# A fused pre-norm transformer block: the first norm moved behind the projections of queries, keys and values

## Chip, cores, metric

The kernel runs on one core of one Trainium2 chip. The metric is the device time of one execution in microseconds (us). All data is float32.

## What is computed

A block of attention and feed-forward over 16 sequences of 256 tokens with 256 features and 16 heads of 16.

```python
def _layernorm(x, axis=-1, eps=1e-05):
    m = jnp.mean(x, axis=axis, keepdims=True)
    v = jnp.var(x, axis=axis, keepdims=True)
    return (x - m) / jnp.sqrt(v + eps)

# attention, on xn = _layernorm(x); heads of 16
q, k, v = (xn @ wq.T), (xn @ wk.T), (xn @ wv.T)            # split into 16 heads
scores = einsum('bihd,bjhd->bhij', q, k) * 16 ** -0.5
scores = where(j - i > 16, -inf, scores)
x = x + einsum('bhij,bjhd->bihd', softmax(scores), v) @ wo.T

# feed-forward, on xn = _layernorm(x); gate_w, up_w (1024 x 256) and down_w (256 x 1024)
# are cubic splines through 2033 control points each
x = x + (silu(xn @ gate_w.T) * (xn @ up_w.T)) @ down_w.T
```

## The kernel before

One sequence is one block of work ("block b": 256 tokens as two chunks of 128 partitions). The main loop (L647) runs over 20 stages `s`. Stage `s` overlaps five blocks: in it the maxima of the scores are searched for block `nb = s - 1`, the exponentials are made for `tb = s - 2`, attention is finished and projected for `ob = s - 3`, the feed-forward part is done for `s - 3` and `s - 4`, and the projections of queries, keys and values are made ahead of need: in stages from 4 on for block `s + 2`, and in stages 0 to 3, where the pipeline fills, by a table (`projections`, L599) that names stage and gap.

A stage has four `inner` and two `outer` steps that multiply queries and keys into two PSUM tiles (`scores`), which DVE (`find_max`, tiles `z` and `mx`) and ACT (`e`, exponentials) read. Between them are gaps numbered 1 to 7, and other work is put into the gaps: `project(s, gap)` for the norm and the projections, `fill(s, gap)` for the feed-forward products (`pg`, `pu`, `pd`) and, in stages 0 to 3, for making the dense weights from the splines (`pw`) and for idle products (`run`, `keep_running`) that only keep TensorE running.

Every engine executes in the order in which the program is written: `InOrder` (L78) records each instruction with that demand, so all of them carry L88 in the profile, and the reader goes by tile names. SP's queue of DMAs is held to the same order: a DMA that waits holds those behind it.

The first norm of block b goes through these steps:

- `load_x` (L126) brings the block in, tile `x`, ten buffers.
- `stats_a` (`norm_stats`, L191): mean and variance on DVE (`statsa`, `mva`), the power -1/2 on GpSimd (`rstda`).
- `norm_a` (L228): two DVE instructions subtract the mean and multiply (`xna`).
- `turn_a` (L231, `transposed`, L212): four TensorE transposes into a PSUM tile (`pta`), and one ACT copy to SBUF (`xnT`).
- `project_qk` (L235): eight matmuls (16 records in the profile) into `pq` and `pk`; ACT copies them to `qkc`, the queries scaled by 16 ** -0.5.
- `spread` (L252): eight DMAs move `qkc` to the layout `qk` that the score products read, four heads at 32-row offsets. Block 0's go half by SP and half by ACT, all others by SP.
- `project_v` (L262): four matmuls into `pv`, two ACT copies into `v`.

When all maxima of a block are found, `turn_max` (L387) transposes them (`pm`, `mxT`), and four DMAs write them as an extra row into `qk`; the products for the exponentials of the next stage subtract the maxima through that row. Every stage of the attention's end has DMAs on SP as well: sums (`den`), heads (`ac`), reciprocals out and back in 16 copies (`rd`, `rb`).

The PSUM tiles tagged `m` have two buffers; `pta`, `pq`, `pk`, `pv`, `po`, `py`, `ptf` (the second norm's transposes) and `pm` take turns in them.

Of the kernel before, what the change touches and what calls it, by code (L numbers as in the profile page):

```python
# [18 lines left out]
P = 128  # L19
# [74 lines left out]
def block_kernel(  # L94
    ctx: ExitStack,
    tc: tile.TileContext,
    x: bass.AP,
    wqT: bass.AP,
    wkT: bass.AP,
    wvT: bass.AP,  # L100
# [11 lines left out]
    const = ctx.enter_context(tc.tile_pool(name="const", bufs=1))  # L112
    sb = ctx.enter_context(tc.tile_pool(name="sb", bufs=2))
    sb1 = ctx.enter_context(tc.tile_pool(name="sb1", bufs=1))
    sb4 = ctx.enter_context(tc.tile_pool(name="sb4", bufs=4))
    sb6 = ctx.enter_context(tc.tile_pool(name="sb6", bufs=6))
    sbx = ctx.enter_context(tc.tile_pool(name="sbx", bufs=10))
# [5 lines left out]

    xs = {}

    def load_x(b, engine):  # L126
        xs[b] = sbx.tile([P, 2, DIM], F32, tag="x", name=f"x{b}")
        engine.dma_start(xs[b], x[b].rearrange("(c p) d -> p c d", p=P))

    AHEAD = 2  # L130
    load_x(0, sp)
    w_in = {}
    for nm, src in (("q", wqT), ("k", wkT), ("v", wvT), ("o", woT)):
        t = const.tile([P, 2, DIM], F32, tag=f"w{nm}", name=f"w{nm}")
        act.dma_start(t, src.rearrange("(kc p) o -> p kc o", p=P))
        w_in[nm] = t
    load_x(1, sp)
    tab_in = const.tile([P, NPART + 2 * P], F32, tag="tab", name="tab_in")
    sp.dma_start(tab_in, tab)
    cp_in = const.tile([P, 3, NPART], F32, tag="cp", name="cp_in")  # L140
    second_in = const.tile([P, 2, NROW], mybir.dt.uint8, tag="second", name="second_in")
    for w in range(3):
        sp.dma_start(cp_in[:, w, :], cps[w])
        if w == 0:
            load_x(2, sp)
            sp.dma_start(second_in, second)
    load_x(3, sp)


    ident = const.tile([P, P], F32, tag="ident", name="ident")  # L150
    make_identity(nc, ident)
    neghalf = const.tile([P, 2], F32, tag="neghalf", name="neghalf")
    pool.memset(neghalf, -0.5)
    mask0 = const.tile([P, JB], F32, tag="mask0", name="mask0")
    mask1 = const.tile([P, S], F32, tag="mask1", name="mask1")
    masks = (mask0, mask1)
# [26 lines left out]
    downT = const.tile([P, 8, DIM], F32, tag="downT", name="downT")  # L183


    xns, xnTs, mxs, aus, aos, recs, x2s, x2Ts = ({} for _ in range(8))
    es, inters, qkcs = {}, {}, {}

    moments = {}
# [1 line left out]
    def norm_stats(b, nm):  # L191
        stats = sb.tile([P, 2, 6], F32, tag=f"stats{nm}", name=f"stats{nm}{b}")
        mv = sb.tile([P, 2, 2], F32, tag=f"mv{nm}", name=f"mv{nm}{b}")
        for c in range(2):
            dve.bn_stats(stats[:, c, :], xs[b][:, c, :])
            dve.bn_aggr(mv[:, c, :], stats[:, c, :])
        rstd = sb.tile([P, 2], F32, tag=f"rstd{nm}", name=f"rstd{nm}{b}")
        dve.tensor_scalar_add(rstd, mv[:, :, 1], EPS)
        pool.tensor_tensor(rstd, rstd, neghalf, ALU.pow)
        moments[b, nm] = mv, rstd  # L200

    def normed(b, nm):
        mv, rstd = moments.pop((b, nm))
        xn = sb.tile([P, 2, DIM], F32, tag=f"xn{nm}", name=f"xn{nm}{b}")
        for c in range(2):
            dve.tensor_scalar(
                xn[:, c, :], xs[b][:, c, :], mv[:, c, 0:1], rstd[:, c : c + 1],
                ALU.subtract, ALU.mult,
            )
        return xn  # L210
# [14 lines left out]
    def stats_a(b):  # L225
        norm_stats(b, "a")

    def norm_a(b):  # L228
        xns[b] = normed(b, "a")

    def turn_a(b):  # L231
        xnTs[b] = sb.tile([P, 2, S], F32, tag="xnT", name=f"xnT{b}")
        transposed(xns.pop(b), xnTs[b], f"ta{b}")

    def project_qk(b):  # L235
        qkcs[b] = qkc = sb.tile([P, 2, 2, S], F32, tag="qkc", name=f"qkc{b}")
        for i, nm in enumerate("qk"):
            pq = ps_m.tile([P, 2, S], F32, tag="m", name=f"p{nm}{b}")
            for oc in range(2):
                for kc in range(2):  # L240
                    pe.matmul(
                        pq[:, oc, :],
                        lhsT=w_in[nm][:, kc, oc * P : (oc + 1) * P],
                        rhs=xnTs[b][:, kc, :],
                        start=(kc == 0),
                        stop=(kc == 1),
                    )
            act.activation(
                qkc[:, i], pq, AF.Copy, scale=HD**-0.5 if nm == "q" else 1.0
            )  # L250

    def spread(b):  # L252
        qkc = qkcs.pop(b)
# [8 lines left out]
    def project_v(b):  # L262
        pv = ps_m.tile([P, 2, DIM], F32, tag="m", name=f"pv{b}")
        for c in range(2):
            for kc in range(2):
                pe.matmul(
                    pv[:, c, :],
                    lhsT=xnTs[b][:, kc, c * P : (c + 1) * P],
                    rhs=w_in["v"][:, kc, :],
                    start=(kc == 0),  # L270
                    stop=(kc == 1),
                )
        for c in range(2):
            act.copy(
                vs[b % NQK][:, c, :, 0:HD],
                pv[:, c, :].rearrange("p (h d) -> p h d", d=HD),
            )
        del xnTs[b]

# [41 lines left out]
    def inner(nb, tb, g):  # L323
# [11 lines left out]
            scores(qt, False, g, 0, 0, S)  # L335
        def exponentials(pr):
            e = sb6.tile([P, 2, S], F32, tag="e0", name=f"e0{tb}_{g}_{pr}")
            act.activation(e, tiles[pr][:, :, 0:S], AF.Exp)

            pool.affine_select(  # L340
                out=e[:, :, 0:M0], in_=e[:, :, 0:M0],
                compare_op=ALU.is_ge, fill=0.0, base=LOOK,
                pattern=[[0, 2], [1, M0]], channel_multiplier=-1,
            )
            es[tb, 0, g, pr] = e
# [7 lines left out]
    def outer(nb, tb, g2):  # L353
# [10 lines left out]
        def exponentials(pr):  # L364
# [4 lines left out]
                    :, :, :, W0 - W1 : W0  # L369
                ],  # L370
                AF.Exp,
            )
            pool.affine_select(
                out=e[:, :, :, 0:P], in_=e[:, :, :, 0:P],
# [95 lines left out]
        norm_stats(b, "f")  # L470

    def norm_f(b):
        x2s[b] = normed(b, "f")

    def turn_f(b):
        x2Ts[b] = sb.tile([P, 2, S], F32, tag="x2T", name=f"x2T{b}")
# [79 lines left out]
    def do(stage, b, *args):  # L556
        if 0 <= b < B:
            stage(b, *args)

    heads = {
        (0, 7): (0, 6),
        (1, 1): (1, 0), (1, 4): (1, 2), (1, 5): (1, 2), (1, 6): (0, 5), (1, 7): (0, 5),
        (2, 1): (1, 0), (2, 3): (1, 6), (2, 5): (1, 1), (2, 6): (0, 4),
        (3, 3): (0, 5), (3, 6): (0, 6),
    }
    parts = iter([(w, part) for part in range(2) for w in range(2)] + [(2, 0), (2, 1)])

    def keep_running(n):
        run = ps_f.tile([P, 2 * S], F32, tag="f", name="run")
# [2 lines left out]

    def fill(s, gap):

        n, idle = heads.get((s, gap), (0, 0))
        if idle:
            keep_running(idle)  # L580
        for _ in range(n):
            spline(*next(parts))

        alone = s > B
        late = s >= B - AHEAD
        for what, at in (
            ((gate_up, s - 4, 1), 1),
            ((gate_up, s - 4, 2), 2 if late else 3),
            ((gate_up, s - 4, 3), 3 if late else 4),
            ((down, s - 4, 0), 4 if alone else 5),  # L590
            ((down, s - 4, 1), 5 if alone else 6),
            ((gate_up, s - 3, 0), 7),
        ):
            if at == gap:
                do(*what)

    projections = {  # L599
        (0, 1): ((stats_a, 1),),  # L600
        (0, 2): (
            (norm_a, 1), (coefficients, 0), (coefficients, 1), (stats_a, 2),
            (scores_and_values, 1), (scores_and_values, 2), (project_qk, 0), (spread, 0),
        ),
        (0, 4): ((turn_a, 1), (norm_a, 2)),
        (0, 6): ((project_v, 0),),
        (1, 1): ((turn_a, 2), (coefficients, 2)),
        (1, 2): ((project_qk, 1), (spread, 1)),
        (1, 3): ((project_qk, 2), (spread, 2), (scores_and_values, 3)),
        (1, 6): ((project_v, 1),),  # L610
        (1, 7): ((stats_a, 3), (norm_a, 3), (project_v, 2)),
        (2, 1): ((turn_a, 3), (stats_a, 4), (scores_and_values, 4)),
        (2, 2): ((norm_a, 4), (project_qk, 3), (spread, 3)),
        (2, 4): ((turn_a, 4),),
        (2, 6): ((project_v, 3),),
        (2, 7): ((stats_a, 5), (norm_a, 5), (project_qk, 4)),
        (3, 1): ((turn_a, 5), (stats_a, 6)),
        (3, 2): ((norm_a, 6), (spread, 4), (project_qk, 5), (spread, 5)),
        (3, 3): ((project_v, 4),),
        (3, 4): ((turn_a, 6),),  # L620
        (3, 6): ((project_v, 5),),
    }

    def project(s, gap):
        if s < 4:
            todo = projections.get((s, gap), ())
        else:
            pb = s + AHEAD
            todo = {
                1: ((stats_a, pb + 1),),  # L630
                2: ((norm_a, pb + 1), (project_qk, pb), (spread, pb)),
                4: ((turn_a, pb + 1),),
                6: ((project_v, pb),),
            }.get(gap, ())
        for stage, b in todo:
            do(stage, b)


    for t in tiles:
# [2 lines left out]
    scores_and_values(0)  # L642
    constants()
    stats_a(0)
    norm_a(0)
    turn_a(0)
    for s in range(B + 4):  # L647
        nb, tb, ob = s - 1, s - 2, s - 3
        inner(nb, tb, 0)
# [4 lines left out]
        inner(nb, tb, 1)  # L654
        do(invert, ob)
        if s + 2 + AHEAD < B:
            load_x(s + 2 + AHEAD, sp)
        project(s, 2)
        fill(s, 2)
        outer(nb, tb, 0)  # L660
# [7 lines left out]
        inner(nb, tb, 3)  # L668
        do(project_o, ob)
        do(stats_f, ob)  # L670
        fill(s, 5)
        do(norm_f, ob)
        outer(nb, tb, 1)
        fill(s, 6)
        do(turn_f, ob)
        project(s, 6)
        do(turn_max, nb)
        project(s, 7)
        fill(s, 7)
# [29 lines left out]
```

## Time and profile before

| | us |
|---|---|
| median of 3 runs | 671.82 (671.68 to 675.86) |
| profiled execution | 670.9 |
| its span, first to last instruction | 669.2 |
| busy: TensorE / weight loads / VectorE / ScalarE / GpSimd | 652.2 / 511.6 / 358.5 / 230.3 / 128.1 |

The span begins with the first instruction and ends with the last, so the execution's time is a little longer. PE is TensorE's matmuls, PEld its weight loads, DVE VectorE, ACT ScalarE, POOL GpSimd, SP the engine that issues most DMAs (SPq is its queue). A row `349.93 0.59 PE pta L88 x4` of the chain of waits is start, duration, engine, tile, line, number of records; in the timeline the operation and its tiles follow. In the table by stretches of time the columns are stretch, length, and for PE, PEld, DVE, ACT and POOL busy time and instructions, then TensorE's granted clock, the share of the DMA engines, and GB/s.

### The profile page before, as it was taken

What the parts mean: (1) busy time and instruction counts of PE and PEld (TensorE: products, weight loads), DVE (VectorE), ACT (ScalarE), POOL (GpSimd) and SP (SyncE); (2) the same over time, 40 slices, a digit from 0 to 9 for tenths busy, and PEclk for the clock granted to TensorE, in tenths of its full rate; (3) what the DMA queues carried; (4) which work ended last, traced back from release to release, by engine and by line L of the source; (5) the groups of instructions that cost most, each with busy time, mean ns of one, the idle gap of its engine ahead of it and who ended that gap; (6) DMA issues with size and microseconds to landing.
All of it is one profiled execution on the core that took longest, in us unless ns stands there. A gap on an engine that the chain in (4) does not pass through costs nothing.

```text
span 669.2 us, 18583 instructions
## 1 busy us (share of the span) xinstructions
PE 652.2 (97%) x7484; PEld 511.6 (76%) x7484; DVE 358.5 (54%) x1473; ACT 230.3 (34%) x413; POOL 128.1 (19%) x250
## 2 busy tenths in 40 slices
PE   7999989999999999999999999999999999999998
PEld 6666767877778787777878777787877777776876
DVE  6576556556464645645464564545455565623332
ACT  2345434243342424334242433423233333333110
POOL 5222212111121211112121121211112121212000
PEclk9999999999999999999999999999999999999999
DMA  8422142113030210313031121303010101010100
GB/s 253 64 40 35 37 82 61 35 23 66 24 77 19 66 33 20 65 27 73 20 72 27 22 63 27 59 19 62 22 30 24 25 14 36 18 45 24 34 17 16
DMA packets 34422, 29.65 MB, mean 44 GB/s; under 512 B 7840, under 2 KB 33696, under 8 KB 34336
## 3 DMA queue, kind: packets, MB, share of 16 engines
q1 hardware_dynamic: 32928, 27.15, 18.1%
q10 hardware_dynamic: 1408, 1.31, 0.7%
q8 instruction: 59, 0.97, 0.6%
q14 instruction: 27, 0.22, 0.1%
HBM read 10.88 MB, written 4.46 MB: 23 GB/s over the span
## 4 chain that ended last, share of the span: by engine, by line
PE 94%; ACT 2%; DVE 2%; DMA 1%; issue 1%; POOL 0%; SPq 0%; ACTq 0%; DVEq 0%
PE pg L88 18%; PE pd L88 17%; PE pu L88 17%; PE scores L88 14%; PE po L88 6%; PE pq L88 5%; PE py L88 5%; PE pk L88 4%; PE pv L88 4%; PE pta L88 1%; PE ptf L88 1%; PE run L88 1%; PE pw L88 1%; ACT e L88 1%; DMA qk<-qkc 1%
## 5 line engine op out<-in xcount | busy, mean ns | idle before, releaser
L88 ACT ACTIVATE e<-scores 128x512 f32<-128x512 f32 (+1 forms) x192 | 117.4, 615 | 252.2 <-PE scores L88 188.5
L88 DVE CUSTOM_DVE_ANT_0 z<-scores,mask 128x144 bf16<-128x144 f32 (+1 forms) x512 | 154.4, 362 | 71.4 <-PE scores L88 36.7
L88 POOL TENSOR_SCALAR_AFFINE_SELECT e<-e 128x224 f32<-128x224 f32 (+1 forms) x192 | 94.6, 493 | 421.4 <-ACT e L88 420.9
L88 PE MATMUL pg<-x2T,gateT 128*128 128x256 f32 x512 | 125.1, 387 | 2.8 <-ACT x2T L88 2.8
L88 PE MATMUL pu<-x2T,upT 128*128 128x256 f32 x512 | 121.0, 379 | 0.0
L88 PE MATMUL pd<-downT,inter 128*128 128x256 f32 x512 | 117.0, 382 | 0.0
L88 DVE SCALAR_TENSOR_TENSOR th<-th,pg 128x512 f32<-128x512 f32 x64 | 44.0, 687 | 132.7 <-ACT th L88 132.7
L88 PEld LDWEIGHTS pg<-x2T,gateT 128*128 128x128 f32 x512 | 92.3, 190 | 21.2 <-ACT x2T L88 4.2
L88 PE MATMUL scores<-qk 17*64 17x144 f32 (+7 forms) x4096 | 105.7, 317 | 2.2 <-ACT e L88 1.1
L88 PEld LDWEIGHTS pu<-x2T,upT 128*128 128x128 f32 x512 | 97.3, 190 | 13.2
L88 PEld LDWEIGHTS pd<-downT,inter 128*128 128x128 f32 x512 | 96.1, 190 | 14.0 <-issue 0.2
L88 PEld LDWEIGHTS scores<-qk 17*64 17x64 f32 (+1 forms) x4096 | 68.6, 131 | 37.8 <-issue 29.2
L88 ACT ACTIVATE th<-pg 128x512 f32<-128x512 f32 x64 | 38.2, 597 | 69.7 <-PE pg L88 69.2
L88 DVE TENSOR_TENSOR inter<-th,pu 128x512 f32<-128x512 f32 x64 | 44.0, 688 | 26.1 <-PE pu L88 26.1
L88 PE MATMUL po<-e,v 128*32 128x256 f32 (+1 forms) x1024 | 50.0, 335 | 0.1
L88 PEld LDWEIGHTS po<-e,v 128*32 128x32 f32 x1024 | 29.6, 109 | 23.3 <-issue 12.5
L88 DVE DVE_READ_ACCUMULATOR2_ANT mx<- 128x1 f32 x512 | 42.2, 82 | 0.0
L88 DVE TENSOR_TENSOR x<-x,pd 128x256 f32<-128x256 f32 x32 | 13.5, 421 | 51.9 <-PE pd L88 51.9
L88 PE MATMUL pq<-xnT,wq 128*128 128x256 f32 x128 | 31.9, 392 | 1.2 <-ACT xnT L88 0.7
L88 PE MATMUL py<-wo,ac 128*128 128x256 f32 x128 | 31.8, 391 | 1.1 <-ACT e L88 1.1
L88 PE MATMUL pv<-wv,xnT 128*128 128x256 f32 x128 | 30.6, 382 | 0.8 <-ACT v L88 0.6
L88 PEld LDWEIGHTS py<-wo,ac 128*128 128x128 f32 x128 | 23.1, 189 | 9.5 <-issue 4.6
(54 smaller groups left out, 414.7 us busy)
## 6 DMA issues: line engine op xcount, KB each, us to landing
qk<-qkc SPq DMA_DIRECT2D x124, 64.0 KB
x<-x SPq DMA_DIRECT2D x16, 256.0 KB
ac<-au SPq DMA_DIRECT2D x128, 32.0 KB
rb<-rd SPq DMA_DIRECT2D x32, 128.0 KB
out<-x SPq DMA_DIRECT2D x15, 256.0 KB
qk<-mxT SPq DMA_DIRECT2D x64, 4.0 KB
den<-au SPq DMA_DIRECT2D x64, 4.0 KB
cp_in<-cps SPq DMA_DIRECT2D x3, 256.0 KB
```

Of the source, the lines that this page charges most:

```text
L88: return self.tc.keep_in_program_order(fn(*args, **kwargs))
```

## The change

With `xn = (x - m) * r`, a projection `xn @ w.T` equals `r * (x @ wc.T)`, where `wc` is `w` with the mean over its input features taken off. So the changed kernel multiplies the raw input with centred weights, and brings in `r` later:

- The host also gives `xT`, each block transposed. `load_xT` fetches it, three buffers, and `norm_a` and `turn_a` are gone for blocks 1 to 15. Block 0 alone keeps norm and transposes (`norm_first`) and uses the weights as they are.
- `sum_weights` multiplies each of the three weights with a matrix of 1/256 (the column means, spread over all partitions), `center` takes them off in place on DVE.
- Values: the ACT copy takes the token's factor as its scale. Queries and keys: tokens lie along the free axis, so `r` is needed in all partitions. `send_factors` writes it to DRAM (`ra`, 128 x 2 single numbers), `spread_factors` reads it back into all partitions (`fa`, 128 x 256), and DVE multiplies `pq` and `pk` by it, in place of ACT's copies.
- The scale 16 ** -0.5 moves into the exponentials.
- The table of stages 0 to 3 is written anew, with idle products and spline parts in it; in stage 3 `project_v` comes ahead of `turn_f`.

```diff
+    sb3 = ctx.enter_context(tc.tile_pool(name="sb3", bufs=3))
...
+    def load_xT(b):
+        xTs[b] = sb3.tile([P, 2, S], F32, tag="xT", name=f"xT{b}")
+        sp.dma_start(xTs[b], xT[b].rearrange("(kc p) t -> p kc t", p=P))
...
+    sp.dma_start(cp_in[:, 0, :], cps[0])
+    load_x(2)
+    load_xT(1)
+    sp.dma_start(second_in, second)
+    sp.dma_start(cp_in[:, 1, :], cps[1])
+    load_xT(2)
+    load_x(3)
+    sp.dma_start(cp_in[:, 2, :], cps[2])
...
+    def norm_first():
+        xTs[0] = sb3.tile([P, 2, S], F32, tag="xT", name="xT0")
+        transposed(normed(0, "a", "f"), xTs[0], "ta0")
...
+    def sum_weights(nm):
+        sums[nm] = ps_f.tile([P, DIM], F32, tag="f", name=f"sum{nm}")
+        for kc in range(2):
+            pe.matmul(
+                sums[nm], lhsT=means, rhs=w_in[nm][:, kc, :], start=(kc == 0), stop=(kc == 1)
+            )
+    def center(nm):
+        for kc in range(2):
+            dve.tensor_tensor(
+                w_in[nm][:, kc, :], w_in[nm][:, kc, :], sums[nm], ALU.subtract
+            )
+    def send_factors(b):
+        _, factors[b] = moments.pop((b, "a"))
+        across[b] = dr.tile([S], F32, tag="ra", name=f"ra{b}")
+        sp.dma_start(across[b].rearrange("(c p) -> p c", p=P), factors[b])
+    def spread_factors(b):
+        to = sb3.tile([P, S], F32, tag="fa", name=f"fa{b}")
+        sp.dma_start(to, across[b].unsqueeze(0).to_broadcast([P, S]))
+        across[b] = to
     def project_qk(b):
...
-                        rhs=xnTs[b][:, kc, :],
+                        rhs=xTs[b][:, kc, :],
...
-            act.activation(
-                qkc[:, i], pq, AF.Copy, scale=HD**-0.5 if nm == "q" else 1.0
-            )
+            if b == 0:
+                act.copy(qkc[:, i], pq)
+            else:
+                dve.tensor_tensor(
+                    qkc[:, i], pq, across[b].unsqueeze(1).to_broadcast([P, 2, S]), ALU.mult
+                )
     def project_v(b):
...
-            act.copy(
+            act.activation(
                 vs[b % NQK][:, c, :, 0:HD],
                 pv[:, c, :].rearrange("p (h d) -> p h d", d=HD),
-            )
+                AF.Copy,
+                scale=1.0 if b == 0 else factors[b][:, c : c + 1],
+            )
...
-            act.activation(e, tiles[pr][:, :, 0:S], AF.Exp)
+            act.activation(e, tiles[pr][:, :, 0:S], AF.Exp, scale=HD**-0.5)
...
+    early = {
+        (0, 1): ((stats_a, 1), (send_factors, 1)),
+        (0, 2): (
+            (project_qk, 0), (spread, 0), (center, "q"), (sum_weights, "k"), (coefficients, 0),
+            (stats_a, 2), (scores_and_values, 1), (scores_and_values, 2),
+        ),
+        (0, 6): (
+            (project_v, 0), (sum_weights, "v"), (center, "k"), (center, "v"), (keep_running, 1),
+            (spread_factors, 1), (send_factors, 2), (spread_factors, 2),
+        ),
+        (1, 1): ((part, 0), (coefficients, 1)),
+        (1, 2): ((project_qk, 1), (spread, 1)),
+        (1, 3): ((project_qk, 2), (spread, 2), (coefficients, 2), (scores_and_values, 3)),
+        (1, 4): ((keep_running, 2), (part, 1)),
+        (1, 5): ((keep_running, 2), (part, 2)),
+        (1, 6): ((keep_running, 5), (project_v, 1)),
+        (1, 7): (
+            (stats_a, 3), (send_factors, 3), (spread_factors, 3), (keep_running, 4),
+            (project_v, 2), (keep_running, 1),
+        ),
+        (2, 1): ((part, 3), (stats_a, 4), (send_factors, 4), (scores_and_values, 4)),
+        (2, 2): ((project_qk, 3), (spread, 3), (spread_factors, 4)),
+        (2, 3): ((keep_running, 6), (part, 4)),
+        (2, 5): ((keep_running, 1), (part, 5)),
+        (2, 6): ((keep_running, 4), (project_v, 3)),
+        (2, 7): ((stats_a, 5), (send_factors, 5), (spread_factors, 5), (project_qk, 4)),
+        (3, 1): ((stats_a, 6),),
+        (3, 2): ((spread, 4), (project_qk, 5), (spread, 5), (send_factors, 6)),
+        (3, 3): ((keep_running, 5), (project_v, 4)),
+        (3, 4): ((spread_factors, 6),),
+        (3, 6): ((keep_running, 4), (project_v, 5)),
+    }
...
+        for stage, b, at in (
+            (stats_a, pb + 1, 1),
+            (project_qk, pb, 2),
+            (spread, pb, 2),
+            (send_factors, pb + 1, 2),
+            (spread_factors, pb + 1, 4),
+            (project_v, pb, 6),
+        ):
+            if at == gap:
+                do(stage, b)
...
-    norm_a(0)
-    turn_a(0)
+    sum_weights("q")
+    norm_first()
     for s in range(B + 4):
...
         if s + 2 + AHEAD < B:
-            load_x(s + 2 + AHEAD, sp)
+            load_x(s + 2 + AHEAD)
+        if 3 <= s + 1 + AHEAD < B:
+            load_xT(s + 1 + AHEAD)
         project(s, 2)
...
+        if s == 3:
+            project(s, 6)
         do(turn_f, ob)
-        project(s, 6)
+        if s != 3:
+            project(s, 6)
```

## Prediction

> **What bounds the kernel now.** I read the page's busy times and slices first, then the chain that ended last, then the timeline of the SP queue for the first 100 us, because the change lives off that queue.
>
> ```profile
> PE 652.2 (97%) x7484; PEld 511.6 (76%) x7484; DVE 358.5 (54%) x1473; ACT 230.3 (34%) x413; POOL 128.1 (19%) x250
> PE   7999989999999999999999999999999999999998
> PE 94%; ACT 2%; DVE 2%; DMA 1%; issue 1%; POOL 0%; SPq 0%; ACTq 0%; DVEq 0%
> ```
>
> TensorE is the bound: busy 97%, 94% of the chain. DVE has room (54%), so work moved to it is free wherever it doesn't hold a TensorE buffer. From stage 4 on the chain is matmuls without a gap; one stage with a transpose of the first norm, and the table by stage:
>
> ```profile
> 334.47 1.92 PE pg L88 x8
> ...
> 348.44 1.49 PE po L88 x32
> 349.93 0.59 PE pta L88 x4
> 350.51 1.73 PE pg L88 x8
> ...
> 176.80:215.60 38.80, 38.80 (x474) 30.78 (x466) 21.39 (x92) 13.97 (x25) 7.43 (x14) 1.00 0.20 44
> 448.90:487.40 38.50, 38.50 (x470) 30.48 (x462) 19.76 (x85) 13.46 (x24) 6.69 (x13) 1.00 0.18 37
> ```
>
> The transposes (`pta`) take 0.59 us, but the `pg` behind them takes 1.73 instead of the 1.92 that it takes directly behind `po`: what goes is 0.59 - 0.19 = 0.40. The second window is stage 13, which has no transpose left to do, and shows it: `pv` to `pv` is 481.70 - 443.22 = 38.48 there, 38.87 in the stages before it.
>
> The SP queue, and TensorE at the end of stage 1:
>
> ```profile
> 12.86 2.96 SPq L88 DMA_DIRECT2D qk<-qkc  x4
> 25.51 11.10 SPq L88 DMA_DIRECT2D qk<-qkc  x16
> 39.64 2.33 SPq L88 DMA_DIRECT2D qk<-mxT  x4
> 82.49 12.02 SPq L88 DMA_DIRECT2D qk<-qkc  x16
> 96.03 2.30 SPq L88 DMA_DIRECT2D qk<-mxT  x4
> 36.75 1.89 PE L88 MATMUL pv<-wv,xnT 128*128 128x256 f32 x8
> 42.47 1.04 PE L88 MATMUL scores<-qk 16*64 16x208 f32 x32
> ```
>
> The 16 spreads of blocks 1 and 2 cost SP 11.1 us (0.69 each) and are done at 36.6; the maxima of block 0 (`qk<-mxT`) follow, and the scores of stage 2, which need both, start at 42.5 without a wait. That free stretch of SP from 25.5 is what the change takes away.
>
> **What the Trainium skill says.** "DMA: Bandwidth & Descriptors", Anatomy of one DMA: engines "do not wait on semaphores"; the wait is on the issuing sequencer, so one waiting DMA holds all behind it. The trace agrees: SP stands still between the rows above. The same section gives about 2 us of fixed cost per DMA; here the last spread leaves SP at 15.8 and the scores that need it start at 17.48 (1.6 us). Its Specifications say that pieces under 512 B are read, modified and written; no row here has 4-byte pieces. "TensorE: Matmul & The Clock Gate", Part 1: after an idle window of some 3.4 us the array runs at half clock until it was busy for as long. Before has no such gap after its start, where 24 `run` records take 4.37 us (0.18 each) against 1.28 for 10 later (0.13), which fits.
>
> **The change, part by part.** I count in the time of before; a lead or lag is against the same instruction there.
>
> *Steady stages 4 to 12.* Gone: 4 transposes, an ACT copy (0.59), two DVE `xna` (0.41 each). ACT's two `qkc` (0.60 each) become DVE multiplications, 0.69 each (row `x<-x,py`, 128x512 with one side in PSUM; I take the same for the broadcast operand; bounds 0.6 to 0.8). They fit: `pq` ends at 341.0, DVE is free at 341.17; `pk` ends at 342.7, done by 343.5; the next maxima start at 344.01. New on SP: `xT` (0.45) and `ra` (0.6) around the spreads, `fa` (0.65) after `ra` has landed. SP is done at 352.1 before and has nothing until 365.5, so some 4 us more are hidden. Factors in `v` copies and the scale in Exp ride on ACT instructions that exist: 0. Gain 9 x 0.39 = **-3.5 us**.
>
> *Stage 0.* Six sums of weights (2 records each, 0.22) and six centring subtractions on DVE (0.42, row `x<-x,pd`) lie where TensorE waits for the spread. But SP issues `xT3` before the spread of block 0, into the buffer of `xT0`, which `pv0` reads last (14.8): the four SP spreads run 15.4 to 18.2 instead of 12.86 to 15.8. The first scores need two of them and start near 18.4 (17.48 before); without the 0.59 of transposes behind them, and with a third coefficient product now between maxima on DVE, stage 1 ends up some **+0.4 us** late (0 to 1.5). `fa1` and `fa2` land near 21.5 to 24 and 25 to 27, before DVE needs them (24.1 and 28.0).
>
> *Stage 1 to 2: the trap.* The pool has three `xT` buffers. The built program has `xT4`'s load on SP in stage 1 ahead of all spreads of blocks 1 and 2, and it waits for the last `pv` of block 1 (`xT1`'s last reader, gap 6). In before that `pv` ends at 38.65; now T = 39.05. From there SP issues: `xT4` 0.5, 16 spreads 11.1, the first maxima 0.6; landing 1.9 (1.6 from the spread above; at most 2.4, as a maxima DMA issued by 96.6 is used at 99.0). T + 14.1 = 53.15. TensorE has `pm`, `pv2` and fillers until T + 3.6, then waits: the first product with block 0's maxima row was at 42.8. **+10.4 us** with the 0.4 of stage 0 in it (9.5 to 11.5). It idles 10 us, so by the clock page it restarts at half clock. My estimate from it: some 4 us of products at twice their time, two thirds of it beside ACT and DVE: **+1.3** (0 to 3).
>
> *Stages 2 and 3.* In stage 2 TensorE waited for the ACT copy `xnT` (45.03 to 45.6) before `pw`; without it `pw`, the two `upT` copies and `pq3` come 1.4 earlier, and later on ACT is free 0.6 earlier: by `pq4` **-1.6** (-1 to -3). In stage 3 the 0.4 per transposes is lost again, since SP's line from `den` to `rb` decides when `ac` is multiplied (86.0) and `py` starts. Then SP again: 16 spreads end at 94.5 before; `xT6` 0.45 ahead of them, `ra6` 0.6 behind, a wait for its landing of 1.9 (as any small DMA; my bound for 4-byte pieces is twice that, 4) and `fa6` 0.65 put the maxima of block 2 at 98.0 instead of 96.03. They land at 100.5, needed at 99.0: **+1.5** (0 to 3.6).
>
> Sum: 10.4 + 1.3 - 1.6 + 1.5 - 3.5 = **+8.1 us**. The profiled execution took 670.9 (span 669.2), 0.9 below the median shown; 679.0 against it, 679.9 against 671.8.
>
> **Rivals.** (a) *A lighter stall*: TensorE restarts warm, stage 3's SP has slack, stages 2 and 3 win back 3: 10.4 - 3 + 0.5 - 3.5 = +4.4, 676.2. For it: only nearest rows price landing and clock. Against: the 11.1 us of issue are measured and can't shrink. (b) *A heavier one*: 4-byte pieces take 4 us to land, so `fa6` and the maxima are 2.1 later, and `fa3` arrives 1.4 after DVE wants it: 683.4. For it: broadcasts are slow here (`rb` leaves SP at 345.7, DVE still waits for it at 350.2). (c) *Not slower*: SP passes `xT4`'s load before 29.2 (= 42.8 - 1.9 - 0.6 - 11.1), so that the spreads still fit: the buffer would have to be free before `pv1`. Then only 0.4 - 1.6 + 1.5 - 3.5 = -3.2 remains, 668.6; with stage 3 hidden too and larger savings there, 664. For it: TensorE is the bound and sheds work in every stage. Against: the program's order and its wait say otherwise.
>
> **How the numbers follow.** Forecast 0.46, (a) 0.28, (b) 0.17, (c) 0.09. Likeliest: 679.9. The range 674.5 to 684.5 leaves out most of (c) and the tails. 1% (6.7 us, about what this kernel's measurement can tell) lies at 678.5 and 665.1: slower takes (b) and nearly all of the forecast, 0.62; same takes (a) and most of (c), 0.33; faster 0.05.
>
> **What would show it.** In the profile after: SP without a DMA from about 23 to 39, then 16 spreads in a row; TensorE's slices 2 and 3 (33 to 67 us) drop by some 10 us in sum; scores of stage 2 released by `qk<-mxT` near 53; the next matmuls slow for some 4 us; `pv` to `pv` 38.5 in stages 4 to 12; a wait for `qk<-mxT` of 1 to 2 us at stage 4. The prediction is wrong if spreads of block 1 leave SP before `pv1` ends, if steady stages do not fall to 38.5, or if new waits of DVE on `fa` show in them.

## The result and the profile after

The changed kernel takes 709.47 us (median of 6 runs, 707.14 to 712.01) beside 674.36 for the kernel before (671.68 to 675.86): a ratio of 1.0529, 95% interval 1.0493 to 1.0564, +35.1 us. The forecast was 679.9. Its sign was right and its size was not. The profiled execution took 708.78, its span is 707.0, 37.8 longer than before.

The page after: busy time of TensorE, its slices, its clock, and the chain that ended last.

```profile
PE 669.8 (95%) x7422; PEld 518.4 (73%) x7422; DVE 368.9 (52%) x1479; ACT 208.2 (29%) x368; POOL 126.9 (18%) x251
PE   7695997799999999999999999999999999999998
PEclk9695797799999999999999999999999999999999
PE 82%; DMA 2%; ACT 1%; SPq 1%; DVE 1%; issue 0%; ACTq 0%; DVEq 0%
```

From slice 9 on (141 us) the page looks as before. All is lost in the first eight slices, in which the table of stages 0 to 3 runs, and their low digits come with low digits of the clock. TensorE is busy 17.6 us longer with 62 records fewer, so part of the loss is slow products, and the rest is waiting. Its mean granted clock is 0.958 over the span of 707.0 us, 1.000 before; that is some 59 us at half clock ((1 - 0.958) x 2 x 707.0).

The steady stages did what was forecast. Below are the products of values of two successive stages in TensorE's timeline, and the chain at the place where `pta` stood:

```profile
442.48 1.89 PE L88 MATMUL pv<-wv,xT 128*128 128x256 f32 x8
480.96 1.89 PE L88 MATMUL pv<-wv,xT 128*128 128x256 f32 x8
...
349.04 1.49 PE po L88 x32
350.53 1.92 PE pg L88 x8
```

`pv` to `pv` is 38.48, the forecast's number; `pg` stands directly behind `po` and takes 1.92.

Timeline of SP after (start, and duration of the issue; rows of a kind are drawn together with the waits between them):

```profile
10.44 0.37 SPq L88 DMA_DIRECT2D ra<-rstda  x1
15.62 8.12 SPq L88 DMA_DIRECT2D qk<-qkc  x4
23.84 0.53 SPq L88 DMA_DIRECT2D fa<-ra  x1
24.47 0.38 SPq L88 DMA_DIRECT2D ra<-rstda  x1
32.47 0.33 SPq L88 DMA_DIRECT2D fa<-ra  x1
48.52 0.37 SPq L88 DMA_DIRECT2D xT<-xT  x1
49.00 10.24 SPq L88 DMA_DIRECT2D qk<-qkc  x16
59.34 2.33 SPq L88 DMA_DIRECT2D qk<-mxT  x4
95.12 0.36 SPq L88 DMA_DIRECT2D ra<-rstda  x1
103.60 0.34 SPq L88 DMA_DIRECT2D fa<-ra  x1
```

Two things are to be seen. The foreseen one is that `xT4` leaves SP at 48.52, right after the last product of `pv1`, and the 16 spreads and the maxima stand behind it in a row. The other is the time from the issue of `ra` to that of `fa`, which waits for its landing: 8.0 and 8.5 us, where the forecast took 1.9. The four spreads of block 0, behind `ra1`, take 8.12 instead of 2.96. SP's waits for `ra` are, in total, times and longest:

```profile
SPq L88 <- DMA ra<-rstda: 88.9, 14, 8.4
```

TensorE at six places:

```profile
23.76 1.25 PE L88 MATMUL scores<-qk 16*64 16x208 f32 x16 [7.59 <-DMA qk<-qkc]
46.60 1.89 PE L88 MATMUL pv<-wv,xT 128*128 128x256 f32 x8
61.14 1.82 PE L88 MATMUL scores<-qk 17*64 17x208 f32 x24 [7.11 <-DMA qk<-mxT]
66.69 3.78 PE L88 MATMUL pq<-xT,wq 128*128 128x256 f32 x8
...
109.86 3.78 PE L88 MATMUL pv<-wv,xT 128*128 128x256 f32 x8 [3.65 <-DVE qkc L88]
...
137.63 1.82 PE L88 MATMUL scores<-qk 17*64 17x208 f32 x24 [3.25 <-DMA qk<-mxT]
```

Before, the first scores, `pq3` and `pq4` run at full clock and without a long wait:

```profile
17.48 0.68 PE L88 MATMUL scores<-qk 16*64 16x208 f32 x12 [0.43 <-DMA qk<-qkc]
47.69 1.99 PE L88 MATMUL pq<-xnT,wq 128*128 128x256 f32 x8
66.18 1.99 PE L88 MATMUL pq<-xnT,wq 128*128 128x256 f32 x8 [0.52 <-ACT v L88]
```

Read as lags against before:

| | before | after | late by |
|---|---|---|---|
| first scores of stage 1 | 17.48 | 23.76 | 6.3 |
| `pv1` | 36.75 | 46.60 | 9.9 |
| first products with block 0's maxima | 42.50 | 61.14 | 18.6 |
| `pq4`, end of stage 2 | 66.18 | 92.16 | 26.0 |
| `py` of stage 3 | 86.81 | 119.58 | 32.8 |
| `pq6` of stage 4 | 105.78 | 147.22 | 41.4 |
| end of the span | 669.2 | 707.0 | 37.8 |

Behind `pq4` the lag grows by the two waits shown last, each with slow products behind it. The first is for DVE's `qkc` of block 5. The second is for the maxima of block 2, which stand behind `ra6` and `fa6` on SP; the forecast had 1 to 2 us for it. The 3.6 won back after stage 4 are the nine shorter stages.

### The profile page after: what moved, and what is told of

It reads as the page before. It is cut to its first block, busy times and chain, and to the rows that moved or that the text cites. A ratio compares the mean times of both kernels' runs of the same rounds, so it can differ in the third digit from the quotient of the medians.

```text
span 707.0 us, 18506 instructions
## 1 busy us (share of the span) xinstructions
PE 669.8 (95%) x7422; PEld 518.4 (73%) x7422; DVE 368.9 (52%) x1479; ACT 208.2 (29%) x368; POOL 126.9 (18%) x251
## 4 chain that ended last, share of the span: by engine, by line
PE 82%; DMA 2%; ACT 1%; SPq 1%; DVE 1%; issue 0%; ACTq 0%; DVEq 0%
PE pg L88 17%; PE pd L88 16%; PE pu L88 15%; PE scores L88 13%; PE po L88 6%; PE py L88 4%; PE pq L88 3%; PE pv L88 3%; PE pk L88 3%; SPq L88 1%; DMA ra<-rstda 1%; PE ptf L88 1%; ACT e L88 1%; DMA qk<-mxT 1%; ACT x2T L88 0%
## 5 line engine op out<-in xcount | busy, mean ns | idle before, releaser
L88 ACT ACTIVATE e<-scores 128x512 f32<-128x512 f32 (+1 forms) x192 | 117.7, 616 | 313.3 <-PE scores L88 238.2
L88 DVE CUSTOM_DVE_ANT_0 z<-scores,mask 128x144 bf16<-128x144 f32 (+1 forms) x512 | 154.5, 362 | 68.7 <-PE scores L88 60.3
L88 POOL TENSOR_SCALAR_AFFINE_SELECT e<-e 128x224 f32<-128x224 f32 (+1 forms) x192 | 93.3, 487 | 448.6 <-ACT e L88 448.2
L88 PE MATMUL scores<-qk 17*64 17x144 f32 (+7 forms) x4096 | 113.8, 329 | 21.5 <-DMA qk<-mxT 10.4
L88 PE MATMUL pg<-x2T,gateT 128*128 128x256 f32 x512 | 127.4, 392 | 2.9 <-ACT x2T L88 2.8
L88 PE MATMUL pu<-x2T,upT 128*128 128x256 f32 x512 | 121.8, 381 | 0.0
L88 PEld LDWEIGHTS scores<-qk 17*64 17x64 f32 (+1 forms) x4096 | 72.1, 135 | 61.9 <-issue 38.5
L88 PE MATMUL pd<-downT,inter 128*128 128x256 f32 x512 | 117.0, 382 | 0.0
L88 DVE SCALAR_TENSOR_TENSOR th<-th,pg 128x512 f32<-128x512 f32 x64 | 44.0, 688 | 132.3 <-ACT th L88 132.3
L88 PEld LDWEIGHTS pg<-x2T,gateT 128*128 128x128 f32 x512 | 93.1, 191 | 24.1 <-DVE mx L88 5.0
L88 PEld LDWEIGHTS pu<-x2T,upT 128*128 128x128 f32 x512 | 98.0, 191 | 13.6
L88 PEld LDWEIGHTS pd<-downT,inter 128*128 128x128 f32 x512 | 96.1, 190 | 14.0 <-issue 0.2
L88 ACT ACTIVATE th<-pg 128x512 f32<-128x512 f32 x64 | 38.3, 598 | 70.6 <-PE pg L88 70.2
L88 DVE TENSOR_TENSOR inter<-th,pu 128x512 f32<-128x512 f32 x64 | 44.1, 689 | 26.9 <-PE pu L88 26.9
L88 PE MATMUL po<-e,v 128*32 128x256 f32 (+1 forms) x1024 | 54.0, 355 | 0.0
L88 PEld LDWEIGHTS po<-e,v 128*32 128x32 f32 x1024 | 30.9, 115 | 26.4 <-issue 16.1
L88 DVE DVE_READ_ACCUMULATOR2_ANT mx<- 128x1 f32 x512 | 42.6, 83 | 0.1
L88 DVE TENSOR_TENSOR x<-x,pd 128x256 f32<-128x256 f32 x32 | 13.5, 422 | 51.1 <-PE pd L88 51.1
L88 PE MATMUL pq<-xT,wq 128*128 128x256 f32 x128 | 35.5, 425 | 1.4 <-ACT v L88 0.7
L88 PE MATMUL pv<-wv,xT 128*128 128x256 f32 x128 | 32.3, 397 | 3.6 <-DVE qkc L88 3.6
L88 PEld LDWEIGHTS pq<-xT,wq 128*128 128x128 f32 x128 | 25.2, 207 | 11.2 <-issue 4.4
L88 PE MATMUL pk<-xT,wk 128*128 128x256 f32 x128 | 31.8, 393 | 0.0
```

What stands on the lines that cost most here:

```text
L88: return self.tc.keep_in_program_order(fn(*args, **kwargs))
```

## The experiments

Each ran beside the kernel before on the same chip; its median there was 673.3 to 675.0, and ratios are against it.

**What the slow `ra` costs.** After the result two theories stood. Theory A: the landing of `ra` was mis-sized, and this is the main loss, either because SP waits for it ahead of `fa` (A1) or because a slow `ra` holds up other DMAs (A2). Rival B: the wait for the `xT` buffer and the half clock behind it are the main loss. Four kernels: one without `ra`, one with `ra` that nobody waits for, one with six `xT` buffers, and one in which the factors travel as two rows of 512 B.

no_ra:

```diff
-        sp.dma_start(across[b].rearrange("(c p) -> p c", p=P), factors[b])
...
-        sp.dma_start(to, across[b].unsqueeze(0).to_broadcast([P, S]))
+        sp.dma_start(to, once.unsqueeze(0).to_broadcast([P, S]))
```

> The changed kernel without the writes of factors to DRAM (ra): the copies over all partitions (fa) read a row of ones written once at the start, so every factor of queries and keys is 1. All else stays, the three xT buffers too. Theory A (the landing of ra was mis-sized: 6 to 8 us in the trace after instead of 1.9, and SP stands behind it four times in stages 0 to 3): what is left is the forecast's own sum without ra, 10.4 + 1.3 - 1.6 - 3.5 = +6.6 on 672 to 675, so 677 to 684. Rival B (the load of xT4 that waits for pv of block 1, and the half clock after it, are the main cost): it stays above 698.

Measured: 685.1 us, ratio 1.0161 (1.0114 to 1.0207), just above theory A's 677 to 684.

ra_unwaited: the second edit of no_ra alone.

> As no_ara's twin: ra is written as in the changed kernel, but nobody waits for it, since fa reads the row of ones. Theory A1 (the cost is the wait: fa behind ra holds SP): within 3 us of the kernel without ra. Theory A2 (the 256 single numbers of each ra also clog the DMA rings, so that what is issued behind them lands later): 8 to 15 us slower than without ra, with the first scores of stage 1 still near 24 us.

Measured: 705.5 us, 1.0465 (1.0424 to 1.0506). Its first scores:

```profile
23.42 1.32 PE L88 MATMUL scores<-qk 16*64 16x208 f32 x16 [7.34 <-DMA qk<-qkc]
```

No instruction needs `ra`'s numbers here, and the first scores are nearly as late as in after (23.76). So A2 holds, with more than the 8 to 15 that I expected: the write itself costs 20 us by its neighbours (no_ra to ra_unwaited), the wait for it ahead of `fa` another 4 (ra_unwaited to after).

xt_six:

```diff
+    sbt = ctx.enter_context(tc.tile_pool(name="sbt", bufs=6))
...
-        xTs[b] = sb3.tile([P, 2, S], F32, tag="xT", name=f"xT{b}")
+        xTs[b] = sbt.tile([P, 2, S], F32, tag="xT", name=f"xT{b}")
```

> The changed kernel with six xT buffers instead of three, so that no load of xT waits for a pv; ra as it is. Theory A: fa2 frees SP at about 33, spreads of blocks 1 and 2 run 35 to 46 instead of 49 to 59, and stage 2 starts near 52 instead of 61; the other waits for ra stay: 8 to 13 us less than the changed kernel, 696 to 702. Rival B: 20 us or more less, below 690.

Measured: 703.0 us, 1.0407 (1.0354 to 1.046): only 6.5 less than after. SP shows what took the wait's place:

```profile
31.87 0.46 SPq L88 DMA_DIRECT2D xT<-xT  x1
32.75 12.53 SPq L88 DMA_DIRECT2D qk<-qkc  x16
...
49.84 0.38 SPq L88 DMA_DIRECT2D ra<-rstda  x1
58.98 0.34 SPq L88 DMA_DIRECT2D fa<-ra  x1
```

The spreads leave early now, but `ra3` takes 9.1, `fa3` is late, and a `pw` in stage 2 waits 3.38 for DVE's `qkc`. So rival B alone, which asked for less than 690, falls.

rows:

```diff
-        across[b] = dr.tile([S], F32, tag="ra", name=f"ra{b}")
-        sp.dma_start(across[b].rearrange("(c p) -> p c", p=P), factors[b])
+        pr = ps_m.tile([2, P], F32, tag="m", name=f"pr{b}")
+        pe.transpose(pr, factors[b], ident)
+        row = sb.tile([2, P], F32, tag="row", name=f"row{b}")
+        act.copy(row, pr)
+        across[b] = dr.tile([2, P], F32, tag="ra", name=f"ra{b}")
+        sp.dma_start(across[b], row)
...
-        (2, 1): ((part, 3), (stats_a, 4), (send_factors, 4), (scores_and_values, 4)),
-        (2, 2): ((project_qk, 3), (spread, 3), (spread_factors, 4)),
+        (2, 1): ((part, 3), (stats_a, 4), (scores_and_values, 4)),
+        (2, 2): ((project_qk, 3), (spread, 3), (send_factors, 4), (spread_factors, 4)),
```

The sends of blocks 1, 3 and 5 move later in the table in the same way, so that the new transposes don't stand ahead of other products.

> The changed kernel with ra written as two rows of 512 bytes: TensorE transposes the 128x2 factors, ACT copies them, SP sends 2x128; sends are put where the factors are ready and behind project_v. Same result, three xT buffers. Theory A: ra lands in some 2 us, as the forecast took it: 679 to 686, the small transposes and copies costing 0.1 us each. Rival B: above 698.

Measured: 686.4 us, 1.0182 (1.0136 to 1.0229). SP in stage 3:

```profile
85.72 0.25 SPq L88 DMA_DIRECT2D ra<-row  x1
86.83 0.34 SPq L88 DMA_DIRECT2D fa<-ra  x1
```

From issue to landing are 1.1 us here and up to 1.7 elsewhere in stages 0 to 3, and 23 us of the loss are gone.

**Places or pieces?** rows changed both. late_ra is rows with the old tile and send, at rows' places:

```diff
-        across[b] = dr.tile([2, P], F32, tag="ra", name=f"ra{b}")
-        sp.dma_start(across[b], row)
+        across[b] = dr.tile([S], F32, tag="ra", name=f"ra{b}")
+        sp.dma_start(across[b].rearrange("(c p) -> p c", p=P), factors[b])
```

> As rows, with the sends at the same places of the table, but with the factors again as 256 numbers of 4 bytes. If the size of the pieces is the cause: each ra takes 6 us or more, fa1 and fa2 come late, DVE waits for them in stage 1; the time is near that of after, 697 to 707. If the places were the cause: near rows, 685 to 689, with the first scores at 19.3.

Measured: 708.3 us, 1.0486 (1.0432 to 1.054). SP waits again (`SPq L88 <- DMA ra<-rstda: 95.9, 15, 8.6`), so the places are not what rows had won by.

**The write by itself.** before_ra is the kernel before with one addition: it writes `rstda` to DRAM at the places where after does, and nobody reads it.

```diff
+        ra = dr.tile([S], F32, tag="ra", name=f"ra{b}")
+        sp.dma_start(ra.rearrange("(c p) -> p c", p=P), factors[b])
```

> The kernel before, which also writes its factors to DRAM as 256 numbers of 4 bytes at the places where after does; nobody reads them. If a slow ra holds up its neighbours by itself: ACT's four spreads of block 0 take 6 or more instead of 2.66, the first scores start near 22 instead of 17.48, later sends hold the spreads of block 3 and the maxima in stages 2 and 3, and the time is 5 to 10 above before. If only a wait for ra costs: the issue of 0.5 each on SP, within 1.5 us of before. Steady stages 38.87 as in before in both cases.

Measured: 689.6 us, 1.0214 (1.0163 to 1.0265): 15 kB of writes that nobody uses cost 14.7 us. That is above my 5 to 10, although the first scores start at 18.97 and not near 22. ACT's queue shows one of the ways:

```profile
14.88 0.63 ACTq L88 DMA_DIRECT2D qk<-qkc  x1
18.45 0.61 ACTq L88 DMA_DIRECT2D qk<-qkc  x1
```

These are ACT's third and fourth spread of block 0. The trace names with each DMA the landing counter that it raises and the one that it waits for. In this program SP and ACT take eight counters in turn, and a DMA waits until the one that used its counter before has landed; the fourth spread has the counter of `ra1`. So a DMA on one queue waits for an unrelated one on another, and its issue at 18.45 tells when `ra1`, issued at 9.60, has landed: the counter is full at 18.43, after 8.8 us. ACT's later copies wait behind that spread.

The counters show a second way, which needs no shared counter. From issue to landing, in us, with pieces of 4 B (before_ra) and of 8 B (before_pairs, below):

| | 4 B | 8 B |
|---|---|---|
| `ra1` | 8.8 | 5.1 |
| SP's load of `x`, issued behind it | 8.6 | 4.9 |
| SP's first spread of block 0 | 5.7 | 3.0 |
| ACT's first spread of block 0 | 5.9 | 3.5 |

None of the last three waits for the counter of `ra1`, and they are issued at nearly the same times in both runs. With 4 B they land after `ra1` all the same (18.61, 18.84 and 19.08), on ACT's queue as on SP's, and TensorE's first scores need these spreads. Why they land behind it, the trace doesn't show. How the 14.7 us divide between the two ways was not measured.

**Number of pieces, or size?** Three variants of that send: the two numbers of a partition side by side (128 pieces of 8 B); one number of each partition (128 pieces of 4 B); mean and variance instead (256 pieces of 8 B).

before_pairs:

```diff
-        sp.dma_start(ra.rearrange("(c p) -> p c", p=P), factors[b])
+        sp.dma_start(ra.rearrange("(p c) -> p c", p=P), factors[b])
```

> As before_ra, but each partition's two numbers lie side by side in DRAM: 128 pieces of 8 B instead of 256 of 4 B, the same bytes. If the time of the send goes by its pieces: about half of the loss of before_ra (14.7), 680 to 684 us, and ACT's four spreads of block 0 some 5 instead of 6 to 9. If it goes by the read-modify-write of a whole DMA whatever its pieces: near 689.

Measured: 674.2 us, 1.0016 (0.9994 to 1.0038).

before_128x4:

```diff
-        sp.dma_start(ra.rearrange("(c p) -> p c", p=P), factors[b])
+        sp.dma_start(ra, factors[b][:, 0:1])
```

> As before_ra (689.6 us, 256 pieces of 4 B) and before_pairs (674.2, 128 pieces of 8 B), but one number of each partition: 128 pieces of 4 B, half the data. If the number of pieces decides: as before_pairs, 673 to 676. If pieces of 4 B are slow whatever their number: above 680, with ACT's four spreads of block 0 near 5.

Measured: 687.0 us, 1.0227 (1.0165 to 1.0289).

before_256x8:

```diff
-        sp.dma_start(ra.rearrange("(c p) -> p c", p=P), factors[b])
+        sp.dma_start(ra.rearrange("c p m -> p c m"), factors[b])
...
-        factors[b] = moments[b, "a"][1]
+        factors[b] = moments[b, "a"][0]
```

> As before_ra, but mean and variance of each token instead of its factor: 256 pieces of 8 B, twice the data. If the number of pieces decides: as before_ra, 686 to 692, ACT's four spreads of block 0 near 5.8. If only pieces of 4 B are slow: as before_pairs, 673 to 676.

Measured: 673.1 us, 1.0006 (0.9979 to 1.0034).

| | 4 B | 8 B |
|---|---|---|
| 128 pieces | +13.7 | +0.5 |
| 256 pieces | +14.7 | -0.2 |

(us against the kernel before beside each.) The size of the piece decides, and the number of pieces hardly matters: ACT's fourth spread leaves at 18.45 with 256 pieces of 4 B and at 18.49 with 128, but at 15.41 and 15.11 with pieces of 8 B:

```profile
18.49 0.59 ACTq L88 DMA_DIRECT2D qk<-qkc  x1
...
15.41 0.61 ACTq L88 DMA_DIRECT2D qk<-qkc  x1
...
15.11 0.61 ACTq L88 DMA_DIRECT2D qk<-qkc  x1
```

My expectation for before_pairs, half of the loss, was wrong: all of it goes. The packets in the traces are as many as the pieces and of their size, and take some 9 ns each, of 4 B as of 8 B; the time passes between them and the landing.

**The wait for the buffer, without the slow write.** rows_six is rows with xt_six's edit.

> The factors travel as two rows of 512 B and xT has six buffers, so that no xT load waits. Theory A (what is left of the loss with rows, 12 us, is the xT4 wait on SP and the half clock behind it): the maxima scores of stage 2 came 12.7 late with rows, pv1 4.1 late; the 8.6 between go, and pq3 is at full clock: 674 us (671 to 678). Rival C (another wait takes its place, as in xt_six, where fa3 did): 680 or more, with DVE waiting for fa in stage 2. If the 2 us of late first scores and the half-clock pq1 are won back later in waits of stages 2 and 3: 670.

Measured: 672.4 us, ratio 0.9973 (0.9954 to 0.9992), 14 less than rows. On SP:

```profile
22.26 0.46 SPq L88 DMA_DIRECT2D xT<-xT  x1
25.94 11.39 SPq L88 DMA_DIRECT2D qk<-qkc  x16
40.16 2.29 SPq L88 DMA_DIRECT2D qk<-mxT  x4
```

The load waits for nothing, and the spreads start nearly as soon as before (25.51). Theory A holds for what was left with rows: it goes with the buffer's wait.

after_pairs and pairs_five ask the same in the changed kernel, with each send at its own place. Each factor is written twice, so pieces have 8 B, and read back as pairs (`n` is 2 below); pairs_five has five `xT` buffers besides.

```diff
+        rstd = sb4.tile([P, 2, n], F32, tag=f"rstd{nm}", name=f"rstd{nm}{b}")
+        dve.tensor_scalar_add(rstd, mv[:, :, 1:2].to_broadcast([P, 2, n]), EPS)
...
+        across[b] = dr.tile([S, 2], F32, tag="ra", name=f"ra{b}")
+        sp.dma_start(across[b].rearrange("(c p) n -> p c n", p=P), factors[b])
...
+        to = sb3.tile([P, S, 2], F32, tag="fa", name=f"fa{b}")
+        sp.dma_start(to, across[b].unsqueeze(0).to_broadcast([P, S, 2]))
+        across[b] = to[:, :, 0]
```

> The changed kernel with each factor written twice, as pieces of 8 B, every send at its place; three xT buffers. fa is read back as 256 pairs, and DVE reads every second number. If 4-byte pieces alone are slow: ra lands in under 3 us, the first scores start near 19 and the time is that of rows, 686 us (683 to 690). If the places of the sends matter as well: 692 or more. DVE's multiplications may grow by reading pairs; 0.65 to 0.69 in after.

Measured: 690.5 us, 1.025 (1.0203 to 1.0296), 19 less than after. The waits of SP for `ra`:

```profile
SPq L88 <- DMA ra<-rstda: 39.0, 13, 3.9
```

These are 3.0 each, so the landing is not as short as with rows. The time lies between my two forecasts, and 4 us stay beside rows; what they consist of was not tested. DVE's multiplications take 0.66 and 0.69 with pairs: no more than before.

> after_pairs with five xT buffers, so that xT4's load waits for nothing. If the buffer's wait is the rest of the loss, as rows_six said: 14 less than after_pairs; without the transposes and copies of rows, steady stages of 38.48 and a little less than rows_six: 670 (667 to 673), under before. If another wait takes its place: 676 or more.

Measured: 674.5 us, 1.0019 (0.9996 to 1.0041), 16 less than after_pairs, but not under before, as I had expected. Its TensorE shows slow products:

```profile
22.07 3.78 PE L88 MATMUL pq<-xT,wq 128*128 128x256 f32 x8
...
88.86 3.75 PE L88 MATMUL py<-wo,ac 128*128 128x256 f32 x8 [1.90 <-issue]
...
96.17 3.00 PE L88 MATMUL pv<-wv,xT 128*128 128x256 f32 x8
```

These three groups take 10.5 us instead of 5.9 (1.99 or 1.89 each at full clock), and `pq6` is 6.4 late at stage 4 (112.15). The steady stages give 3.5 back, and the span is 3.0 longer than before.

**The half clock.** rows_warm is rows with more idle products: 18 records ahead of the first scores and 58 ahead of stage 2.

```diff
-            (send_factors, 1), (send_factors, 2), (spread_factors, 1), (spread_factors, 2),
+            (send_factors, 1), (send_factors, 2), (spread_factors, 1), (spread_factors, 2),
+            (keep_running, 9),
...
-            (spread_factors, 3), (keep_running, 1),
+            (spread_factors, 3), (keep_running, 29),
```

> As rows (three xT buffers, 686.4 us), but idle products cover TensorE's wait before the first scores (18 records) and before the maxima scores of stage 2 (58 records), so that the waits stay and the clock does not fall. If the half clock is a cost of its own: pq1 and pq3 take 1.99 instead of 3.7 to 3.8, and the time falls by 3 to 5 us to 682. If it lies beside DVE, ACT and SP anyway: within 1 us of 686.4.

Measured: 687.6 us, 1.0196 (1.0134 to 1.0257), no gain.

```profile
46.49 6.64 PE L88 MATMUL run<-ident 128*128 128x128 f32 x58
53.06 0.58 PE L88 MATMUL scores<-qk 16*64 16x208 f32 x8
56.88 1.01 PE L88 MATMUL scores<-qk 17*64 17x208 f32 x24 [3.24 <-DMA qk<-mxT]
61.52 3.68 PE L88 MATMUL pq<-xT,wq 128*128 128x256 f32 x8
```

The records were too few. A wait of 3.24 us remained, and the products behind it were slow all the same: the clock is 1.00 until 58, then 0.53 and 0.50 until 64. Shorter waits were enough at the first scores of this run: after waits of 1.55 and 0.51 (scores at 21.49 and 23.76) `pq1` took 3.34 at 24.68, with a clock of 0.63 from 23 to 27. So the 3.4 us of idling that the prediction names is not needed, and the run doesn't tell what the half clock costs.

The other runs on record give an estimate. The 107 runs of the kernel before that stood beside these experiments differ in mean granted clock, and their times go with it: 670.6 us on average at 1.000 (11 runs), 676.6 at 0.992 (12 runs). A mean of 0.992 is 10.8 us at half clock ((1 - 0.992) x 2 x 676.6), and these runs are 6.0 longer. So in the kernel before, half clock is not hidden beside other work: it goes with a loss of about half its length. The waits that bring it on are in that figure too.

**A better version?** best is rows_six with `turn_f` ahead of `project_v` in stage 3 too, four idle products there, and numbers instead of rows from block 7 on.

```diff
-        if s == 3:
-            project(s, 6)
         do(turn_f, ob)
-        if s != 3:
-            project(s, 6)
+        project(s, 6)
...
-        (3, 4): ((spread_factors, 6),),
+        (3, 4): ((spread_factors, 6), (keep_running, 4)),
```

> rows_six with three edits: the second norm's transposes of stage 3 again ahead of the values' product (with rows_six the first gate product there started at 95.81 and ran at half clock, 2.77 instead of 1.89, after a wait of 1.63), four idle products in stage 3 before the wait for ac, and single numbers instead of rows from block 7 on, where they are hidden. Expected: first gate product of stage 3 at 94 to 95 and at full clock, 2 to 3 less there; steady stages 38.48 instead of 38.59, 1 less in all: 669.5 us (667 to 672), 0.5 to 1% under before. If the half clock and the order lie beside other work again, as with rows_warm: 671.5 to 672.5.

Measured: 671.9 us, ratio 0.9971 (0.9954 to 0.9987): as rows_six. Its profiled execution had half clock at `pq1` and at a `pv` in stage 3:

```profile
22.10 3.78 PE L88 MATMUL pq<-xT,wq 128*128 128x256 f32 x8
...
96.39 3.40 PE L88 MATMUL pv<-wv,xT 128*128 128x256 f32 x8
```

rows_six and best are 0.3% faster than before, all that the change has brought here. At equal clock it is more. With a mean clock of 0.995, best took 670.6 (5 runs) and the kernel before beside it 675.2 (12 runs); with 0.992 they took 672.6 (10) and 676.9 (3). That is 4.3 to 4.6 us, the forecast's 3.5 of the steady stages and a little more. But the median run of best is at 0.992 and that of before at 0.997, so part of it goes again to half clock, which in the profiled execution lies in stages 1 and 3.

## Why the prediction was right in its sign and wrong in its size

- **Right: the bound and the steady stages.** 38.48 per stage, nine stages, 3.5; DVE's multiplications 0.65 and 0.69; no stall on `fa` there, although `ra` lands late: it is hidden.
- **Right: the wait for the `xT` buffer.** It sits where the text put it. From the end of `pv1` (48.5) to the scores with maxima are 12.6 in after, 14.1 in the forecast: the spreads left SP in 10.24 instead of 11.1, and the maxima landed sooner. By lags it added 8.7 (18.6 - 9.9) where I had 10.0. The sum started from 42.8 for the first product with maxima; the trace has 42.50.
- **Wrong: "a wait for its landing of 1.9 (as any small DMA; my bound for 4-byte pieces is twice that, 4)".** This is the step that failed. The trace of before has no 4-byte pieces, and I took the nearest small DMA as their price and doubled it as a bound. `ra6`, which that term was about, took 6.7 from issue to landing, and the five before it took 8.0 to 11.8 (`ra1` from 10.44 to 22.2, when ACT's fourth spread, which waits for it, leaves). The Trainium skill's page "DMA: Bandwidth & Descriptors" (Specifications) says that below 512 B a DMA does read-modify-write; these runs show nearly all of the cost between 8 B and 4 B, since writes in pieces of 8 B cost the kernel before nothing that can be measured and those in pieces of 4 B cost 14 to 15. The fixed 2 us that the prediction quotes from that page (Anatomy of one DMA) are given there for DMAs that GpSimd issues; SP issues these.
- **Wrong with it: where the cost was looked for.** The sum held `ra` as a wait of SP ahead of `fa6` alone, and rival (b) added 2.1 and 1.4 for `fa`. ra_unwaited and before_ra show that most of it falls on DMAs that have nothing to do with `ra`: those issued behind it land after it, on both queues, and those that share its landing counter wait for it. A term of +1.5 measured 19 (after to after_pairs) to 23 (after to rows). None of the three signs of being wrong that the prediction names came: they looked at the spreads of block 1 and at the steady stages, and the loss lay elsewhere.
- **Undersized: what follows the stall.** The forecast had +10.4, and +1.3 for half clock behind this one wait. Taking the buffer's wait away gave 14 (rows to rows_six) and 16 (after_pairs to pairs_five). Over the 8.7 of the wait, 5 to 7 lie in what followed, slow products (`pq3` 3.78 instead of 1.99) among them. How much of it is clock was not separated, since rows_warm did not keep the clock up. In all, after spent some 59 us at half clock, behind several waits.
- **Half there: the -1.6 of stages 2 and 3.** Where nothing stalls it shows: rows_six has `pq3` 1.6 earlier than before (46.07), `pq4` 0.8 (65.38) and `py` of stage 3 0.9 (85.91). Behind that it is lost: `py` takes 3.03 and the first `pg` 2.77, both slow, and `pq6` is 2.4 late (108.23).
- **Rival (c)**, not slower if the load passes SP early: rows_six is that case with the write mended. It comes out 2.4 under before, where (c) had 3.2. With the slow write left in (xt_six) it is 28 above.

So two terms make up the loss: 709.5 less 19.0 (4-byte pieces) less 16.0 (buffer and what follows) is pairs_five's 674.5, which can't be told from the kernel before. Each is measured with the other in that order; with the slow write still there, the buffers were worth only 6.5 (xt_six).

## What to carry to other kernels

An operation that the profile of before does not show has no nearest row: its upper bound is then what the schedule can bear, not twice a small neighbour, and a change that rests on it is worth one run of the old kernel with that operation alone. A slow DMA is charged to its neighbours: here those issued behind it landed after it, on both queues, and the eighth behind it waited for its landing counter. So look at what is urgent behind it, and not only at who needs its data. A load placed ahead of urgent sends needs a buffer that is free by then: five buffers instead of three were worth 16 us here, once the slow write was gone.

## What the runs showed that I had not expected

- In stages 0 to 3, writes to DRAM in 4-byte pieces landed 6.7 to 11.8 us after their issue in after, with 128 pieces as late as with 256 (ACT's spread at 18.49 and 18.45). Pieces of 8 B in the same places let that spread go at 15.1 to 15.4; SP waits 3.0 for them in after_pairs. Two rows of 512 B landed after 1.1 to 1.7. What happens between the packets and the landing stays open.
- A wait of TensorE of 3.24 us was enough for half clock, although 58 records had run right ahead of it, and so were waits of 1.55 and 0.51 close together (rows_warm).
